# A residual kept in DRAM by token, read back in overlapping rows, in place of four transposes per tile

## The chip, the cores and the metric

The kernel runs on one core of one Trainium2 chip. The metric is the device time of one execution in microseconds. The kernel before took 4258.75 us (median of three runs, 4256.78 to 4262.93). TensorE is called PE below, its weight loads PEld, VectorE DVE, ScalarE ACT, GpSimd POOL, and SyncE, which issues nearly all DMAs, SP.

## The reference

The input is `u`, four sequences (batches) of 1024 tokens with 128 features, in fp32. Four stages follow one another, each as `x = x + layernorm(stage(layernorm(x)))`: a selective state-space scan (called mamba in the code), a mixture of eight experts of which two are chosen per token, a convolution with weights computed per token (31 taps, 16 heads), and a transformer of six layers. The change lies in the last, whose layer is:

```
for i in range(DEPTH):                                   # 6
    x = attn_layer(shift_tokens(x), Wqkv[i], q_scale[i], k_scale[i], Wo[i]) + x
    x = ffn_layer(shift_tokens(x), ln_g[i], ..., W2[i], b2[i]) + x
```

`shift_tokens` delays the upper 64 features by one token. Attention has 16 heads of 64 and is local: the tokens are cut into windows of 32, and a window's queries see the keys and values of its own window and the one before, 64 rows in all. Queries and keys are normalized, scaled and rotated by position. The feedforward part is a layernorm, two 128 x 341 products, a GELU gate and a product back.

## The kernel before, in words

**What is on the chip.** The residual of a batch is held with features on the partitions and tokens along the free axis, in two tiles of 1,186 columns: `hs[b][0]`, called h0, feeds attention, and `hs[b][1]`, called h1, takes its result and feeds the feedforward part. The upper 64 partitions are stored one column to the right, so that a column read straight down is a shifted token. `halves()` (line 1141) names the two halves.

**Tiles and blocks.** Attention goes by tiles of 128 tokens, four windows each: 8 tiles per batch and layer, 192 in all, in the order batch, layer, tile. The feedforward part goes by blocks of 512 tokens, two per batch and layer, 48 in all.

**A tile's steps.**

- `project` (line 1256) multiplies 128 columns of h0 with the query and key weights (four products of 512 columns). ACT squares the results for the norms; DVE multiplies them by the cosine and sine rows of the tile `rot` into `r` and `rb`, POOL adds the two and scales by the inverse root.
- `turn` (line 1314) transposes queries and keys on PE; ACT copies them out as `qT` and `kT`.
- `scores` (line 1328) forms the products of each window's queries and keys (`kT,qT` in the profile), with the mask added by PE; DVE subtracts the maximum, ACT takes the exponential, POOL divides. The result is `at`.
- `mix` (line 1387) needs the values. The value and output weights are multiplied beforehand (`wvo`), so that attention is applied to the residual rows themselves. For that the rows must have tokens on the partitions. `windows` (line 1373) makes them: it transposes 128 columns of h0 on PE for each of four overlapping pieces, 32 tokens apart, into one PSUM bank (`bank<-ident,hs` in the profile), and ACT copies the bank to the tile `xw`. A piece holds four windows of 32 rows, so its rows 0 to 63 serve the even heads of one window and its rows 64 to 127 the odd heads of another; for the first two windows of a tile these are pieces of the tile before, which `mix` gets as `before`. In the first tile of a layer there is no such tile, and two further pieces are turned. Then `at` is transposed to `aT`, the products `aT,xw` (16 instructions a tile) give `zT`, and the products `zT,wvo` (32 instructions) give the attention's result, to which DVE adds h0 into h1.

**A block's steps.** `feedforward` (line 1440) transposes four pieces of h1 on PE (also `bank<-ident,hs` in the profile), normalizes, transposes back, forms three pairs of products with GELU tiles `ge` between, and adds the result to h1 into h0 for the next layer.

**What else runs.** The stages before the transformer for batches 1 to 3 (`mamba`, `chosen_experts`, `conv`) and the preparation of layers 1 to 5 (`prepare_layer`) run beside the tiles, each paced by the number of the tile (`Line`, line 1603). `conv` ends with `finish` (line 1118), which normalizes, transposes and writes h0 for layer 0, for batch 0 one tile at a time and for the others four.

**Order of the work.** Instructions are not issued as the Python code runs. `Order` (line 145) records them as units, finds what depends on what (DRAM by ranges too), and `arrange` (line 278) lays out a schedule with a cost for each kind of unit: 2 us and bytes at 180 GB/s for a DMA, 0.11 us for a transposed piece, and so on. At each step it gives out the unit that can start earliest on its engine, and among those that can start within a short time of it (1 us for DMAs) the one first in program order. It looks ahead by 500 units and assigns the seven shared PSUM banks. Each engine then executes its own list strictly in that order and waits at its head. SP's list holds the DMAs from all stages. All work is recorded in `take` and issued in `give`, so nearly every instruction of the profile has one line, L374; instructions are told apart by their tiles.

**Buffers named below.** `rot` has three buffers, loaded by `load_rot` (line 1237) one tile before its `project`; `xw` two; `ge` two; `eT`, which carries the value and output weights of `prepare_layer` to DRAM, one. `rows` (in DRAM) holds the convolution's input by token; its 30 leading rows are set to zero at the start, in `Common.__init__`, by copies from a zero tile (`rows<-exs` in the profile, the tile being named after its ring). Behind them the same tile fills the experts' lists `listed`, 2.9 MB.

The main loop is `run` (line 1501): `ahead(i + 2)` projects a tile two iterations early, `mix` runs one iteration behind `scores`.

## Time and profile before

| What | Value |
|---|---|
| median of three runs | 4258.75 us (4256.78 to 4262.93) |
| profiled execution, its own time | 4259.06 us |
| its span, first to last instruction | 4257.2 us |
| mean granted TensorE clock | 0.948 |
| PE busy | 3801.6 us |
| DVE busy | 3612.4 us |
| POOL busy | 2964.5 us |
| ACT busy | 2610.7 us |
| bytes moved by DMA | 261.25 MB, 61 GB/s on the mean |

The times are those of one profiled execution. "Busy" counts the time in which an engine executes at least one instruction; matmuls overlap, so that the sum of their durations is more than the busy time, and the time from one group's start to the next group's start tells what a group costs. In a group's line the operands stand as `out<-in`, then shapes and count, then busy time and the mean duration in ns, and behind the bar the idle time of the engine just before these instructions with what ended it. Slices are fortieths of the span, some 106 us each, with a digit for tenths of busy time. In a list of waits a line says which engine, for the instruction that writes the named tile, waited for which engine and tile, with the total in us, the number of times and the longest. `SPq` is SP's list of DMAs. In a timeline a line gives start, duration, engine, operation and tiles, and the count of instructions merged into it.

### The profile page before, as it was taken

What the parts mean: (1) busy time and instruction counts of PE and PEld (TensorE: products, weight loads), DVE (VectorE), ACT (ScalarE), POOL (GpSimd) and SP (SyncE); (2) the same over time, 40 slices, a digit from 0 to 9 for tenths busy, and PEclk for the clock granted to TensorE, in tenths of its full rate; (3) what the DMA queues carried; (4) which work ended last, traced back from release to release, by engine and by line L of the source; (5) the groups of instructions that cost most, each with busy time, mean ns of one, the idle gap of its engine ahead of it and who ended that gap; (6) DMA issues with size and microseconds to landing.
All of it is one profiled execution on the core that took longest, in us unless ns stands there. A gap on an engine that the chain in (4) does not pass through costs nothing. (4 is left out here: it accounts for less than half of the span.)

```text
span 4257.2 us, 112033 instructions
## 1 busy us (share of the span) xinstructions
PE 3801.6 (89%) x45306; PEld 2721.5 (64%) x45317; DVE 3612.4 (85%) x9374; ACT 2610.7 (61%) x4854; POOL 2964.5 (70%) x1832
## 2 busy tenths in 40 slices
PE   3874788998988999988999999999999999999997
PEld 1762465675665666656676677766666777777775
DVE  4668789888997879999998787898989898888985
ACT  3754466675555777655667676666665666666664
POOL 3388667666878766777789665788688666666663
PEclk6886899999998999989999999999999999999998
DMA  3323321222112221111113122121111010101100
GB/s 91 104 83 123 119 85 43 86 62 72 60 68 82 91 73 55 45 57 53 44 63 114 58 65 63 41 73 59 58 61 51 27 41 25 32 21 34 33 27 11
DMA packets 136878, 261.25 MB, mean 61 GB/s; under 512 B 16112, under 2 KB 93992, under 8 KB 129192
## 3 DMA queue, kind: packets, MB, share of 16 engines
q1 hardware_dynamic: 123352, 211.47, 15.0%
q0 software_dynamic: 13008, 42.62, 3.2%
q8 instruction: 357, 5.85, 0.6%
q14 instruction: 161, 1.32, 0.1%
HBM read 224.41 MB, written 29.62 MB: 60 GB/s over the span
## 5 line engine op out<-in xcount | busy, mean ns | idle before, releaser
L374 POOL TENSOR_TENSOR r<-r,rb 128x1024 f32<-128x1024 f32 x384 | 906.9, 2367 | 365.2 <-DVE rb L374 297.9
L374 POOL TENSOR_TENSOR r<-r,root 128x1024 f32<-128x1024 f32 x384 | 723.2, 1903 | 181.2 <-DVE root L374 154.4
L374 PE MATMUL bank<-wqk,hs 128*128 128x512 f32 x1536 | 769.7, 624 | 45.0 <-DVE at L374 13.3
L374 PEld LDWEIGHTS bank<-zT,wvo 128*128 128x128 f32 x6144 | 723.2, 194 | 88.8 <-issue 53.2
L374 PE MATMUL bank<-zT,wvo 128*128 128x128 f32 x6144 | 729.4, 277 | 6.5 <-ACT zT L374 3.5
L374 ACT ACTIVATE sq<-bank 128x512 f32<-128x512 f32 x768 | 450.4, 601 | 458.1 <-DVE words L374 228.1
L374 ACT COPY zT<-bank 128x512 f32<-128x512 f32 x768 | 403.7, 597 | 382.4 <-PE bank L374 376.6
L374 DVE TENSOR_TENSOR r<-bank,rot 128x512 f32<-128x512 f32 x768 | 522.0, 680 | 103.4 <-issue 36.2
L374 POOL TENSOR_TENSOR at<-at,sm 128x1024 f32<-128x1024 f32 x192 | 365.4, 1903 | 326.2 <-DVE sm L374 146.3
L374 DVE TENSOR_TENSOR rb<-bank,rot 128x512 f32<-128x512 f32 x768 | 520.8, 678 | 62.8 <-ACT sq L374 53.8
L374 DVE TENSOR_REDUCE words<-sq 128x8 f32<-128x512 f32 x768 | 526.5, 686 | 14.3 <-ACT sq L374 5.3
L374 PEld LDWEIGHTS bank<-wqk,hs 128*128 128x128 f32 x1536 | 267.6, 195 | 322.7 <-issue 157.7
L374 PE MATMUL bank<-aT,xw 64*128 64x256 f32 x3072 | 430.6, 404 | 25.4 <-DVE at L374 10.3
L374 PE MATMUL bank<-ident,r 128*128 128x128 f32 x3080 | 400.6, 278 | 45.1 <-DVE rb L374 10.0
L374 PEld LDWEIGHTS bank<-ident,r 128*128 128x128 f32 x3080 | 350.1, 143 | 134.9 <-issue 59.7
L374 PEld LDWEIGHTS bank<-aT,xw 64*128 64x128 f32 x3072 | 295.6, 192 | 153.2 <-issue 44.3
L374 PEld LDWEIGHTS bank<-kT,qT 64*32 64x32 f32 x24576 | 259.7, 106 | 106.8 <-issue 105.4
L374 PE MATMUL bank<-kT,qT 64*32 64x64 f32 x24576 | 296.6, 227 | 12.4 <-issue 11.9
L374 DVE TENSOR_REDUCE mx<-bank 128x8 f32<-128x512 f32 x384 | 254.1, 680 | 44.4 <-PE bank L374 44.3
L374 PE MATMUL bank<-fxn,w 128*128 128x512 f32 (+1 forms) x576 | 272.8, 607 | 7.0 <-ACT fxn L374 4.8
L374 ACT ACTIVATE at<-at 128x1024 f32<-128x1024 f32 x192 | 203.5, 1060 | 117.6 <-DVE at L374 83.2
L374 ACT COPY qT<-bank 128x512 f32<-128x512 f32 x384 | 228.3, 600 | 66.2 <-PE bank L374 62.8
(207 smaller groups left out, 6849.8 us busy)
## 6 DMA issues: line engine op xcount, KB each, us to landing
near<-rows SPq DMA_DIRECT2D x31, 1024.0 KB
near<-rows SPq DMA_DIRECT2D x31, 960.0 KB
rot<-rotd SPq DMA_DIRECT2D x192, 128.0 KB
wqk<-in_Wqkv SPq DMA_DIRECT2D x48, 512.0 KB
wvo<-wvod SPq DMA_DIRECT2D x24, 1024.0 KB
ewt<-in_w_ex SPq DMA_DIRECT2D x16, 514.0 KB
w<-in_W SPq DMA_DIRECT2D x24, 341.0 KB
wvod<-eT SPq DMA_DIRECT2D x24, 256.0 KB
```

The source lines that it names most:

```text
L374: getattr(engine, op)(*map(real, args), **{k: real(v) for k, v in kw.items()})
```

## The change

The residual of every layer is also kept in DRAM with one row per token, in a pair of buffers per batch that alternate by layer, with 32 leading rows of zeros. A new function `by_token` turns a block (or a tile, in batch 0 of the convolution's end) once: four transposes on PE into one bank, one ACT copy to a tile `xs` (in the ring of `ge`), one DMA to DRAM. `finish` calls it for layer 0 and `feedforward` for layers 1 to 5. `windows` no longer uses PE and ACT: it reads the four overlapping windows of 64 rows from DRAM, twice, into partitions 0 to 63 and 64 to 127 of `xw`, so that even and odd heads find their own windows and `before` is not needed. It is called for tile i in iteration i, ahead of the mixing of tile i - 1, which uses the `xw` read one iteration earlier. The ring of `rot` goes from three buffers to two. The zero rows of the eight new buffers are filled at the start, between the zero rows of `rows` and the fills of `listed`.

```diff
@@ Common.__init__ @@
+        self.inner = [
+            [dram.tile([WIN + SEQ, D], F32, name=f"inner{b}_{i}") for i in range(2)]
+            for b in range(NB)
+        ]
...
         for rows in self.rows:
             dma(out=rows[:PADL, :], in_=zero[:PADL])
+        for rows in [r for pair in self.inner for r in pair]:
+            dma(out=rows[:WIN, :], in_=zero[:WIN])
@@ Common.finish @@
         for part, dst in halves(self.hs[b][0], j * BLK + ts.start * P, n * P):
             nc.scalar.copy(dst, ps[part][:, : n * P])
+        self.by_token(b, 0, j * BLK + ts.start * P, n)
+
+    def by_token(self, b, l, t0, n):
+
+        c0 = PRE + t0
+        ps = self.transpose4("px", [self.hs[b][0][:, c0 + g * P : c0 + (g + 1) * P] for g in range(n)])
+        xs = self.sb.tile([P, 4, P], F32, "xs", tag="ge", bufs=2)[:, :n, :]
+        self.nc.scalar.copy(xs, ps[:, :n, :])
+        rows = self.inner[b][l % 2][WIN + t0 : WIN + t0 + n * P, :]
+        self.dma(out=rows.rearrange("(g p) d -> p g d", p=P), in_=xs)
@@ Transformer.load_rot @@
-        rot = self.sb.tile([P, 4, DH], F32, "rot", bufs=3)
+        rot = self.sb.tile([P, 4, DH], F32, "rot", bufs=2)
@@ Transformer.windows, mix @@
-    def windows(self, b, t, chunks):
+    def windows(self, b, l, t):
+        xw = self.sb.tile([P, 4, P], F32, "xw", bufs=2)
+        first = self.c.inner[b][l % 2][t * P : t * P + 1, :]
+        src = bass.AP(first.tensor, first.offset, [[D, 2 * WIN], [WIN * D, 4], [1, D]])
+        for e in range(2):
+            self.c.dma(out=xw[e * 2 * WIN : (e + 1) * 2 * WIN], in_=src)
+        return xw
+
+    def mix(self, b, t, at, xw):
         nc, c = self.nc, self.c
-        px = c.bank("px").rearrange("p (g f) -> p g f", f=P)
-        with nc.together(0.11 * len(chunks)):
-            for i, g in enumerate(chunks):
-                c0 = PRE + t * P + (g - 1) * WIN
-                nc.tensor.transpose(px[:, i, :], c.hs[b][0][:, c0 : c0 + P], c.ident)
-        xw = self.sb.tile([P, 4, P], F32, "xw", bufs=2)
-        n = len(chunks)
-        nc.scalar.copy(xw[:, 4 - n :, :], px[:, :n, :])
-        return xw
-
-    def mix(self, b, t, at, before):
-        if before is None:
-            before = self.windows(b, t, (-2, -1))
-        xw = self.windows(b, t, range(4))
...
-                            (xw if e == 0 else xw if g > 1 else before)[rows, (g + 2 * e) % 4, :],
+                            xw[rows, g, :],
@@ Transformer.feedforward @@
+        if l + 1 < DEPTH:
+            c.by_token(b, l + 1, j * BLK, 4)
@@ Transformer.run @@
                 qT = self.turn(projected.pop(i), kT)
+                old, xw = xw, self.windows(b, l, t)
...
-                mixing = self.mix(bm, tm, at, xw if tm else None)
-                xw = next(mixing)
+                mixing = self.mix(bm, tm, at, old if i < len(tiles) else xw)
+                next(mixing)
```

More of the change, by code (lines that the diff above doesn't have):

```diff
@@ L1371, in scores @@
         return at
-    def windows(self, b, t, chunks):
-        nc, c = self.nc, self.c
-        px = c.bank("px").rearrange("p (g f) -> p g f", f=P)
-        with nc.together(0.11 * len(chunks)):
-            for i, g in enumerate(chunks):
-                c0 = PRE + t * P + (g - 1) * WIN
-                nc.tensor.transpose(px[:, i, :], c.hs[b][0][:, c0 : c0 + P], c.ident)
-        xw = self.sb.tile([P, 4, P], F32, "xw", bufs=2)
-        n = len(chunks)
-        nc.scalar.copy(xw[:, 4 - n :, :], px[:, :n, :])
-        return xw
-    def mix(self, b, t, at, before):
-        nc, c = self.nc, self.c
-        if before is None:
-            before = self.windows(b, t, (-2, -1))
-        xw = self.windows(b, t, range(4))
+    def windows(self, b, l, t):
[6 more added lines that the diff above has]
+    def mix(self, b, t, at, xw):
+        nc, c = self.nc, self.c
         aT = self.sb.tile([P, 8, P], F32, "aT", bufs=2)
@@ L1401, in mix @@
             nc.scalar.copy(aT[:, 4 * j : 4 * j + 4, :], pt)
-        yield xw
+        yield
         zT = self.sb.tile([P, 2, 4, 8, WIN], F32, "zT")
@@ L1422, in mix @@
                 )
-        yield xw
+        yield
         py = c.bank("py")
@@ L1437, in mix @@
             nc.vector.tensor_tensor(out=dst, in0=py[rows, :P], in1=src, op=ALU.add)
-        yield xw
+        yield
     def feedforward(self, b, j, l):
```

## The prediction

> **What bounds the kernel now.** I read the page's busy times and slices first, then the windows by stage, then PE's own waits, then the order of time. The page's span, busy line and slices of PE and DVE:
>
> ```profile
> span 4257.2 us, 112033 instructions
> PE 3801.6 (89%) x45306; PEld 2721.5 (64%) x45317; DVE 3612.4 (85%) x9374; ACT 2610.7 (61%) x4854; POOL 2964.5 (70%) x1832
> PE   3874788998988999988999999999999999999997
> DVE  4668789888997879999998787898989898888985
> ```
>
> There are three stretches: a start of 400 us with PE at 4 to 8 tenths, a middle where PE and DVE take turns, and a second half with PE at nine tenths throughout. The view by windows (PE, PEld, DVE, ACT and POOL busy, then the granted clock) puts numbers on the last two:
>
> ```profile
> 400.00:2200.00 1800.00, 1581.26 (x18391) 1112.36 (x18398) 1569.91 (x4063) 1114.38 (x2109) 1317.62 (x827) 0.94 0.21 69
> 2200.00:4150.00 1950.00, 1885.05 (x24521) 1373.55 (x24520) 1717.51 (x4401) 1245.30 (x2266) 1374.17 (x791) 1.00 0.15 49
> ```
>
> From 2200 to 4150 PE is busy 96.7% and DVE 88%; from 400 to 2200 the two are at 88% and 87% and neither bounds alone. PE's own waits from 2200 to 4150 (total, times, longest) are small and scattered:
>
> ```profile
> PE bank L374 <- DVE at L374: 9.2, 11, 2.1
> PE bank L374 <- DVE rb L374: 9.1, 17, 2.1
> PE bank L374 <- ACT qT L374: 8.4, 12, 1.4
> ```
>
> The timeline of PE shows one tile running without a gap, and in it the four pieces that the change removes (`ident,hs`):
>
> ```profile
> 3614.18 1.91 PE L374 MATMUL bank<-ident,r 128*128 128x128 f32 x16
> 3615.93 0.60 PE L374 MATMUL bank<-ident,hs 128*128 128x128 f32 x4
> 3616.37 1.04 PE L374 MATMUL bank<-ident,at 128*128 128x128 f32 x8
> ```
>
> The next group starts 0.44 us after the pieces do; the same gap is 0.44 at 3629.96 and 0.43 at 3645.15. So a set of four costs PE 0.44 us, not the sum of the durations, which overlap.
>
> **The change part by part**
>
> *Turning taken away and put back.* The two groups in question, by form:
>
> ```profile
> L374 PE MATMUL bank<-ident,hs 128*128 128x128 f32 x1008 | 156.5, 280 | 9.5 <-DVE hs L374 3.5 <-DVE at L374 2.2 <-ACT qT L374 1.0
> L374 ACT COPY xw<-bank 128x512 f32<-128x512 f32 x192 | 118.6, 617 | 10.1 <-PE bank L374 8.8 <-DVE rb L374 1.1
> ```
>
> Of 1008 transposes 192 are the feedforward's (48 blocks of 4). The other 816 are the windows: 192 tiles of 4 and 24 first tiles with 2 more. They all go. `by_token` turns each block once per layer: 48 times 4, 192. Net 624 fewer, at 0.44/4 = 0.109 us: 68.0 us of PE at full clock, 0.354 us a tile.
>
> By the number of products `aT,xw` (16 a tile) 78 tiles lie before 2200 us, 109 up to 4150 and 5 behind. Late: 114 tiles by 0.354 is 40.4 us. PE is idle 65 us of those 1950, so nearly every microsecond of PE moves the end; but DVE, at 88%, comes to 90% of the shortened stretch and some waits grow. Bounds 70% and 100%, I take 85%: 34.3 us. Early: 78 by 0.354, at a granted clock of 0.94, is 29.4 us. Here DVE and the chains of other stages hold the end half of the time: bounds 0 and 100%, I take 45%: 13.2 us.
>
> A rule that would forbid this gain: the Trainium skill, "Perfetto Trace Analysis", section "Identifying the Most-Contended Engine", judges TensorE's headroom by the share of its weight loads and not by matmul busy time. By it PE would stand at 1373.55 of 1950, 70%, DVE would be the contended engine, and the sum would be the start's +6 us, against −41.5 by the rows. The gapless tile above speaks for matmul time in this stretch.
>
> *Copies on ACT.* 192 copies (118.6 us) and 24 half ones (9.6) go; 46 of 128x512 at 617 ns and 8 of 128x128 (like `exsT`, 297 ns) come: 97.4 us less on an engine 61% busy. Its waits on PE are its idle time, so I take 0. Bound above: PE's late waits for ACT (about 23 us) vanish. Bound below 0, as ACT's work only shrinks.
>
> *The reads.* 384 reads of 128 KB, two per tile. SP needs 0.32 us for an issue: 384 reads, 54 writes and 8 zero fills are 143 us of an engine that mostly waits. Landing is bounded by the loads of `x` (256 KB in the same 512-byte rows): issued at 0.74 and used at 3.43, 2.7 us; behind megabytes, issued at 14.39 and used at 21.83, 7.4 us. The buffer is free when the products of two tiles before have read it (3607.1) and is needed at 3633.8: 26.7 us of cover against 0.64 + 7.4. I take 0. With the cover gone a read would cost PE what it lies beyond it.
>
> *The write and its read.* The write waits for the ACT copy, the first read for the write's landing. The nearest row: `rows` written at 1056.67, read at 1059.12, 2.45 us, during which SP holds what is queued behind. It follows the block's residual add, whose tile's products come more than a tile (14 us) later; 0 taken, and 48 times 2.45, 118 us, if nothing covered it.
>
> *DMA traffic.* 50.3 MB read and 12.6 MB written, 122,880 packets. The hardware queue now takes 15.0% of 16 engines for 123,352 packets, 0.083 us each; at that rate the share doubles to 30%. Not a bound: 0.
>
> *SP's queue and the rotation ring from three to two.* SP's waits over the whole run:
>
> ```profile
> SPq L374 <- DVE rb L374: 1640.9, 159, 27.8
> SPq L374 <- PE bank L374: 1057.1, 214, 36.3
> ```
>
> SP already stands most of the time before a rotation load that waits for `rb`. With two buffers a load is released by the last `rb` of the tile before (3603.4) and needed by `r` one tile on (3622.4): 19.0 us, where three gave one tile more. Less 0.32 and 7.4, 11.3 us are spare; window reads have 18.7. Behind SP's head stand rotations, weights, windows and the experts' rows; DVE waits for the first, PE for the others. From 3400 on SP's longest wait is 23.6 us. I take 0, since SP's entries follow the planned order of the same events; the bound is a rival below.
>
> *The start.* Eight zero fills come between the four that exist and the large fills. SP's queue and ACT there (start, duration):
>
> ```profile
> 16.11 4.13 SPq L374 DMA_DIRECT2D rows<-exs  x4
> 21.03 5.28 SPq L374 DMA_DIRECT2D listed<-exs  x2
> 26.41 4.42 SPq L374 DMA_DIRECT2D exn<-in_WvT  x1
> ...
> 32.11 5.64 SPq L374 DMA_DIRECT2D wvod<-eT  x2
> ...
> 36.80 0.59 ACT L374 COPY eT<-bank 128x512 f32<-128x512 f32 x1 [17.98 <-DMA wvod<-eT]
> ```
>
> ACT stands 17.98 us before the second `eT`, which waits for a write that SP issues behind these fills; mamba's own copies stand behind it, and PE, DVE and POOL idle. Eight more fills at 0.6 to 1.03 us delay this by 5 to 8 us. Bounds 0 (made good before 400 us) and 8.2; I take +5. In batch 0 `by_token` comes in eight single pieces beside the convolution's chain (hs copied at 243.9, projected from 246.7): +1, bounds 0 and 8 times 0.57 (a transpose and a copy) = 4.6.
>
> **Sum.** −34.3 − 13.2 + 5 + 1 = −41.5 us. The profiled execution took 4259.06 us (span 4257.2 and 1.9 around it), 0.3 above the median of 4258.75; so 4217 us.
>
> **The rivals**
>
> *All of the freed PE time comes back:* −40.4 − 29.4, and at the start +1: 4190. For it: PE's late stretch has no gap and early the copies that go unburden ACT; against it: DVE at 87 and 88%.
>
> *The gain is taken up by DVE:* the freed PE time turns into waits `PE <- DVE at` and `DVE rb`, and only the start's +6 is left: 4265, within the measure. For it: DVE is at 91 to 93% in the windows 1000 to 1300, 1600 to 1900 and 1900 to 2200. Against it: the late stretch, with three fifths of the tiles, where it is at 88%.
>
> *Slower: SP's single queue.* A rotation load or window read is held behind an entry whose engine is late, and DVE's `r` waits for DMA. It decides when holds exceed the spare 11.3 us. If one load in each of the 24 layers meets a hold of the size of SP's longest late wait, 23.6 us, it costs 12.3 us each, 295 us, the far end; if in every third layer, 8 by 12.3 = 98 us against the 41.5 saved: 4315. The point from which it is slower at all is 3.4 such loads. For it: the ring of two, the 1057 us in which SP waits for PE, and one 10.3 us wait of PE for `exs<-listed` already. Against it: no rotation load is waited for anywhere in the trace, though they stand in the same queue.
>
> **How the numbers follow.** A median differing by 0.2% (8.5 us) is about what can be told from no change. The forecast, 4200 to 4240, has 0.50; all of it coming back, below 4200, 0.20; a smaller gain, 4240 to 4250, 0.07; taken up by DVE, 0.09; slower through SP, 0.14. So faster 0.77, same 0.09, slower 0.14. For 8 in 10 the range leaves out a tenth on each side: 4182 (the full gain and some of ACT's 23 us) to 4275 (a little of the third rival); the likeliest case's own is 4200 to 4240.
>
> **What the new profile would show.** Right: `ident,hs` at 384 instructions and PE busy near 3801.6 − 97, as 624 of 1008 rows of 156.5 us go (their overlap counted in); `xw<-bank` gone from ACT, 54 copies to `xs` in its place; tiles of the late stretch 0.35 us closer; the second `eT` at 42 to 45 us. No engine waits on `xw` or `rot` by DMA. Wrong: lines such as `DVE r <- DMA rot` or `PE bank <- DMA xw` with more than some 10 us in total; PE waits on DVE after 2200 us up by 30 or more; or tiles farther apart because the planned order itself differs, which no row of this trace prices and which would break the forecast in either direction.

## The result: 1.4% slower, and the profile after

The changed kernel took 4317.82 us (median of four runs, 4312.42 to 4324.13), the kernel before beside it 4257.76 us (4252.15 to 4262.93): a ratio of 1.0136, 95% interval 1.0118 to 1.0154. Forecast were 4217 us and a range up to 4275. The profiled execution took 4317.51 us. Its span, busy line and hardware DMA queue, from the page of the changed kernel:

```profile
span 4315.7 us, 111685 instructions
...
PE 3805.1 (88%) x44676; PEld 2659.9 (62%) x44693; DVE 3608.5 (84%) x9374; ACT 2547.4 (59%) x4698; POOL 2964.4 (69%) x1832
...
q1 hardware_dynamic: 253624, 274.54, 20.0%
```

There are 630 matmul records fewer, and PE is busy for as long as before (3805.1 us; the forecast had it near 3801.6 − 97). The groups say that the work has gone; what is left of `ident,hs`, the longest group beside it, and SP's new DMAs with their issue times (minimum, median and longest in ns), all of the changed kernel:

```profile
L374 PE MATMUL bank<-ident,hs 128*128 128x128 f32 x384 | 64.9, 286 | 13.8 <-DVE hs L374 7.1 <-ACT hs L374 4.5 <-DVE rb L374 0.8
...
L374 PE MATMUL bank<-wqk,hs 128*128 128x512 f32 x1536 | 788.5, 630 | 39.3 <-DVE at L374 8.9 <-DVE m L374 7.9 <-DVE rb L374 4.8
```

```profile
L374 SPq DMA_DIRECT2D xw<-inner x384: 573/579/1850, 251.9 to 4256.3; - x192
L374 SPq DMA_DIRECT2D inner<-ge x54: 319/382/1266, 250.1 to 4190.2; - x54
L374 SPq DMA_DIRECT2D inner<-exs x8: 302/365/422, 20.0 to 25.3; - x8
```

`ident,hs` lost 91.6 us of records (156.5 before), but the records of the other groups grew: `wqk,hs` by 18.8, `aT,xw` by 21.7, `ident,r` by 9.7. So the busy time of PE did not fall with its work, and does not tell by itself how much room PE has.

The windows by stage (same columns as in the prediction; the cuts after the first are put 60 us later):

```profile
400.00:2260.00 1860.00, 1614.48 (x18379) 1105.02 (x18391) 1595.69 (x4123) 1110.94 (x2079) 1347.40 (x846) 0.93 0.26 82
2260.00:4210.00 1950.00, 1862.04 (x23942) 1326.20 (x23942) 1695.37 (x4358) 1192.93 (x2152) 1346.99 (x776) 0.99 0.21 66
```

In the late 1950 us, where most of the gain was forecast, PE is 23 us less busy than before (1885.05), but the tiles follow no faster, as the table below shows; what PE no longer does, it waits, for several engines (the longest of these waits; total, times, longest; 2260 to 4210 us of the changed kernel):

```profile
PE bank L374 <- POOL at L374: 14.5, 27, 1.7
PE bank L374 <- DVE at L374: 13.7, 14, 3.6
PE bank L374 <- issue: 9.1, 19, 1.6
```

No engine waits for a read of `xw` or for `rot`. The only waits for a new DMA are these two of ACT:

```profile
ACT ge L374 <- DMA inner<-ge: 2.5, 2, 2.2
ACT L374 <- DMA inner<-ge: 2.3, 2, 1.2
```

They look too small to matter, 4.8 us together. They are the trail to the cause. The moment at which each tile's products `zT,wvo` start, read from the traces, shows where the 60 us arise (us behind the kernel before, whose own start is in the second column; "tie alone" and "own buffer" are two of the experiments below):

| tile | before, us | changed kernel | tie alone | own buffer |
|---|---|---|---|---|
| 0 | 428 | -4.9 | +10.3 | -2.2 |
| 30 | 1173 | +11.1 | +6.3 | +7.4 |
| 36 | 1294 | +43.1 | +30.0 | +10.8 |
| 72 | 2091 | +30.9 | -1.5 | +8.2 |
| 78 | 2208 | +42.9 | +23.8 | +5.9 |
| 120 | 3000 | +45.5 | +22.6 | +0.2 |
| 126 | 3116 | +56.5 | +47.8 | -0.8 |
| 186 | 4147 | +60.8 | +54.2 | -5.3 |

The loss comes in steps, near tiles 35, 77 and 124, and between tiles 126 and 186 little changes: none of the gain forecast for these late tiles appears (60 by 0.354 us, 21 us). Part of the first step is made good again: by tile 72 the changed kernel has 12 us of it back, and the tie alone all of it. Against the run with an own buffer the steps are clearer: 32 us at tile 36, 23 at 72, 37 at 78, 45 at 120, 57 at 126 and 66 at 186. Near these tiles three of the six pieces of the convolution for later batches end (`finish`), beside the transformer. (The kernel before runs at slightly different speeds on different chips, medians of 4245 to 4263 us, so the last two columns may hold some 12 us of that by the end; the experiments are compared by ratios to the kernel before on the same chip.)

ScalarE's timeline at the first step names the event (changed kernel; start, duration, operation):

```profile
1241.12 0.69 ACT L374 ACTIVATE ge<-bank,b 128x512 f32<-128x512 f32 x1
1245.71 0.68 ACT L374 ACTIVATE ge<-bank,b 85x512 f32<-85x512 f32 x1 [3.90 <-DVE pd L374]
...
1266.20 1.17 ACT L374 COPY hs<-bank 64x512 f32<-64x512 f32 x2
...
1271.24 0.58 ACT L374 COPY ge<-bank 128x512 f32<-128x512 f32 x1 [1.72 <-PE bank L374]
...
1275.65 1.28 ACT L374 ACT_TABLE_LOAD   x1
1276.95 0.69 ACT L374 ACTIVATE ge<-bank,b 128x512 f32<-128x512 f32 x1
```

Two of the three GELU operations of a feedforward run at 1241 and 1246; the remaining one only at 1277. Between them stands, at 1271.24, a copy into a buffer of the same ring: it is `xs` of the convolution's end, in `by_token`. A ring of two buffers is handed out in program order. Here `xs` stands just ahead of the feedforward's three GELUs (in the 18th feedforward between the first and the second), so the GELU two places behind it, the second of the three, takes the same buffer again. It gets it only after the convolution has transposed, copied `hs`, transposed again, copied `xs` and stored it; the third, 85 wide, takes the other buffer and ran before it. In the view of the waits this is nearly invisible, since the order written out for ACT already has the GELU behind the copy: ACT does other work in between, and nobody is recorded as waiting for it.

### The profile page after: what moved, and what is told of

It is laid out like the page before. It is cut to its first block, busy times and chain, and to the rows that moved or that the text cites. A ratio compares the mean times of both kernels' runs of the same rounds, so it can differ in the third digit from the quotient of the medians.

```text
span 4315.7 us, 111685 instructions
## 1 busy us (share of the span) xinstructions
PE 3805.1 (88%) x44676; PEld 2659.9 (62%) x44693; DVE 3608.5 (84%) x9374; ACT 2547.4 (59%) x4698; POOL 2964.4 (69%) x1832
## 5 line engine op out<-in xcount | busy, mean ns | idle before, releaser
L374 PE MATMUL bank<-wqk,hs 128*128 128x512 f32 x1536 | 788.5, 630 | 39.3 <-DVE at L374 8.9
L374 DVE TENSOR_TENSOR r<-bank,rot 128x512 f32<-128x512 f32 x768 | 524.1, 682 | 117.2 <-PE bank L374 45.5
L374 PE MATMUL bank<-aT,xw 64*128 64x256 f32 x3072 | 452.3, 410 | 44.9 <-DVE at L374 21.8
L374 PE MATMUL bank<-ident,r 128*128 128x128 f32 x3080 | 410.3, 280 | 56.1 <-POOL r L374 25.4
L374 PEld LDWEIGHTS bank<-aT,xw 64*128 64x128 f32 x3072 | 301.4, 194 | 194.9 <-issue 45.1
```

What stands on the lines that cost most here:

```text
L374: getattr(engine, op)(*map(real, args), **{k: real(v) for k, v in kw.items()})
```

## The experiments

Ratios are to the kernel before on the same chip, with 95% intervals. "Tie" means that the convolution's `xs` and the feedforward's GELU share the ring `ge`.

### Where the loss comes from

**The changed kernel with a buffer of the convolution's own for `xs`.**

```diff
-        self.by_token(b, 0, j * BLK + ts.start * P, n)
+        self.by_token(b, 0, j * BLK + ts.start * P, n, "cxT", 1)
...
-    def by_token(self, b, l, t0, n):
+    def by_token(self, b, l, t0, n, tag="ge", bufs=2):
...
-        xs = self.sb.tile([P, 4, P], F32, "xs", tag="ge", bufs=2)[:, :n, :]
+        xs = self.sb.tile([P, 4, P], F32, "xs", tag=tag, bufs=bufs)[:, :n, :]
```

> The changed kernel, but by_token called at the end of the convolution puts xs into the convolution's own buffer cxT instead of the ring ge of the feedforward part. Theory 4, the shared ring ties the side stage's end to the main line's GELU tiles, in an order fixed by the program, and the list of every engine pays for it: some 30 us faster than the changed kernel, a ratio to before near 1.007. Theory 5, the added work itself (turning, copies, DMAs) costs: within 8 us of the changed kernel, ratio 1.012 to 1.014.

Measured: 4250.98 us against 4246.74, ratio 1.0011 (1.0001 to 1.0020). Nearly the whole loss is gone, with all transposes, copies, reads and writes of the change in place. (The order of the instructions is laid out anew here too; more on that below.) The same feedforward's GELUs, in ACT's timeline of this run:

```profile
1237.40 1.26 ACT L374 ACTIVATE ge<-bank,b 128x512 f32<-128x512 f32 x2
1241.99 0.68 ACT L374 ACTIVATE ge<-bank,b 85x512 f32<-85x512 f32 x1 [3.33 <-DVE pd L374]
```

From the first GELU to the last, that feedforward (the 8th of 48) takes 4.6 us here and 35.8 in the changed kernel; the 18th takes 7.9 against 31.4, the 30th 5.7 against 27.1. That is 76 us of stretching in three places, at the three steps of the table. What the held feedforward costs the engines is seen in windows over these three stretches (PE, PEld, DVE, ACT, POOL busy); first the changed kernel, then the run with an own buffer at its corresponding times:

```profile
1245.00:1277.00 32.00, 23.61 (x384) 17.14 (x384) 23.21 (x74) 19.47 (x35) 8.03 (x9) 0.92 0.24 71
2138.00:2162.00 24.00, 19.04 (x235) 13.41 (x236) 18.90 (x82) 16.13 (x31) 7.39 (x8) 0.93 0.18 54
3058.00:3081.00 23.00, 18.28 (x348) 13.12 (x347) 16.75 (x66) 16.94 (x30) 8.64 (x6) 0.97 0.33 102
```

```profile
1241.00:1273.00 32.00, 28.78 (x408) 19.79 (x408) 29.95 (x95) 20.23 (x39) 9.95 (x6) 0.92 0.15 44
2115.00:2139.00 24.00, 21.92 (x232) 14.04 (x232) 23.03 (x80) 15.11 (x28) 10.76 (x8) 0.93 0.15 47
3013.00:3036.00 23.00, 21.32 (x329) 13.90 (x328) 19.71 (x70) 14.39 (x30) 8.12 (x6) 1.00 0.24 70
```

PE is busy 60.9 of 79 us in the changed kernel and 72.0 in the other; DVE 58.9 and 72.7. Layer by layer, the next attention needs the feedforward's result, and while that is held the two engines run out of work. These windows hold only 11 us (PE) to 14 us (DVE) of the loss; more of it follows behind them, when the late layer starts: from the products of tile 33 to those of tile 36 the changed kernel takes 80 us (1257 to 1337), the run with an own buffer 51 (1253 to 1304).

**The kernel before with the tie alone.** The converse, with almost no work: one column of 128 numbers is copied into a buffer of the ring and stored.

```diff
@@ finish, in the kernel before @@
+        tie = self.sb.tile([P, BLK], F32, "tie", tag="ge", bufs=2)
+        nc.scalar.copy(tie[:, :1], ps[:, :1])
+        self.dma(out=self.tied[k], in_=tie[:, :1])
```

> The kernel before, complete, with the tie of the two buffers alone added: at the end of each convolution piece a buffer of the GELU's ring of two is taken, ScalarE copies one column into it and one DMA of 128 x 4 bytes stores it in a DRAM tensor that nothing reads. No rows by token are written or read, the windows are transposed as before. Theory of the tie (the feedforward's GELU waits for the convolution's end because both take the same two buffers in program order): most of the loss comes back, 25 to 65 us over the kernel before, 4283 to 4323 us. Rival (the loss lies in the copies, the rows or the reads, and the own buffer of the earlier run helped only by another order): a few small copies and stores cost 0 to 10 us, 4258 to 4268 us.

Measured: 4306.82 us against 4246.01, ratio 1.0143 (1.0127 to 1.0158). Fourteen copies of 0.16 us and as many stores cost 61 us, as much as the whole change. ACT's timeline at the second step, the store in SP's, and what PE waited for behind it:

```profile
2121.94 1.17 ACT L374 COPY hs<-bank 64x512 f32<-64x512 f32 x2 [0.58 <-PE bank L374]
2123.12 0.16 ACT L374 COPY ge<-bank 128x1 f32<-128x1 f32 x1
...
2132.39 1.28 ACT L374 ACT_TABLE_LOAD   x1 [6.27 <-DMA tied<-ge]
2133.68 0.69 ACT L374 ACTIVATE ge<-bank,b 85x512 f32<-85x512 f32 x1
```

```profile
2123.31 0.33 SPq L374 DMA_DIRECT2D tied<-ge  x1
```

```profile
2134.42 0.80 PE L374 MATMUL bank<-aT,xw 64*128 64x256 f32 x2 [6.31 <-ACT ge L374]
```

Here the hold shows openly: the GELU's table load waits 6.27 us for the store of the tiny tie, the GELU follows, and PE stands 6.31 us. The 8th, 18th and 30th feedforwards take 45.1, 36.3 and 14.9 us between their first and last GELU (4.6, 4.2 and 2.7 in the kernel before). The steps of the table lie at the same tiles as in the changed kernel, but the first, with the longest hold, is made good by tile 72; what stays comes from the other two. Taken away alone and added alone, the tie is worth 53 and 61 us: it is the cause of the loss. That the two amounts are so near each other is not to be read closely. In the tie alone the GELU's table load starts 9.1 us after the issue of the store (2123.31 to 2132.39), in the changed kernel, at its first step, 3.8 us after (1271.85 to 1275.65).

**The changed kernel with three buffers for `rot`.**

```diff
-        rot = self.sb.tile([P, 4, DH], F32, "rot", bufs=2)
+        rot = self.sb.tile([P, 4, DH], F32, "rot", bufs=3)
```

> The changed kernel with three rotation buffers as before. Theory 3, the shorter ring delays rotation loads behind SP's head: most of the 60 us come back, 4260 to 4280. Theories 1 and 2: 4318, within 10.

Measured: 4297.88 against 4245.22, ratio 1.0118 (1.0096 to 1.0140), where the changed kernel had 1.0136. The third buffer brings some 8 us, within the two intervals, and does not explain the loss.

**The kernel before in another planned order.** Its work is complete; the schedule is laid out as if the windows cost nothing.

```diff
-        with nc.together(0.11 * len(chunks)):
+        with nc.together(0.0):
...
-        nc.scalar.copy(xw[:, 4 - n :, :], px[:, :n, :])
+        nc.scalar.copy(xw[:, 4 - n :, :], px[:, :n, :]).cost = 0.0
```

> The kernel before with all of its work, but the planner is told that the window transposes and their copies cost nothing; so only the order of instructions changes, in the way in which the change alters it. Theory 1 (order): it moves by more than 20 us, and slower, 4280 to 4320. Theory 2 (the freed time is worth nothing, order is not the cause): within 10 of 4258.

Measured: 4253.62 against 4245.22, ratio 1.0018 (1.0009 to 1.0028). Leaving the windows out of the plan costs 8 us. The order of the changed kernel itself, which also has the new work in it, is not tested by this.

### What TensorE's freed time is worth

**The kernel before with its windows planned but not issued.** Every other instruction keeps its place; `xw` holds a constant, so the windows are left out.

```diff
-                nc.tensor.transpose(px[:, i, :], c.hs[b][0][:, c0 : c0 + P], c.ident)
+                nc.tensor.transpose(px[:, i, :], c.hs[b][0][:, c0 : c0 + P], c.ident).ghost = True
...
-        nc.scalar.copy(xw[:, 4 - n :, :], px[:, :n, :])
+        nc.scalar.copy(xw[:, 4 - n :, :], px[:, :n, :]).ghost = True
@@ Order.give @@
+            if u.ghost:
+                continue
```

> The kernel before, with its order of instructions kept to the letter: the window transposes and their copies are planned as before but left out when the instructions are issued, and xw holds a constant set once (so attention mixes constants, and the output is not the reference's). Theory 1, the freed time of PE and ACT is worth what the forecast said and the loss comes from the new order: 4190 to 4218 us. Theory 2, the freed time is worth nothing since waits for DVE and POOL end last in every tile: 4245 to 4262.

Measured: 4232.10 against 4245.22, ratio 0.9966 (0.9951 to 0.9982). Leaving out 816 transposes at 0.109 us, 89 us of PE, and the copies on ACT brings 14 us: 16%. The timeline of PE in the late stretch shows what became of the time:

```profile
3591.63 1.91 PE L377 MATMUL bank<-ident,r 128*128 128x128 f32 x16
...
3594.77 1.49 PE L377 MATMUL bank<-kT,qT 64*32 64x64 f32 x128
3596.80 2.00 PE L377 MATMUL bank<-aT,xw 64*128 64x256 f32 x16 [0.54 <-issue]
...
3605.83 1.91 PE L377 MATMUL bank<-ident,r 128*128 128x128 f32 x16
```

In this tile PE stands 0.54 us before `aT,xw`, about what the transposes had cost, and the period from `ident,r` to `ident,r` is 14.20 us: no shorter than the 14.03 us of the tile of the kernel before that the prediction showed (from 3614.18 to the next `ident,r` at 3628.21). Over tiles 110 to 185 the mean period by the two traces is 17.43 us here and 17.44 before. The engine that PE stands for is not named (`issue`), but the windows of the two tiles, first the kernel before, show a second engine that is full:

```profile
3614.18:3628.21 14.03, 14.03 (x216) 11.12 (x215) 13.66 (x33) 9.03 (x17) 11.58 (x8) 1.00 0.04 11
```

```profile
3591.63:3605.83 14.20, 13.66 (x212) 11.00 (x211) 13.71 (x33) 8.52 (x16) 11.63 (x8) 1.00 0.04 12
```

In the tile without a gap on PE, DVE was busy 13.66 of 14.03 us, 97%. The 88% of the late stretch is a mean over tiles like this one and others. Without the transposes PE is busy 13.66 us and DVE 13.71 of the 14.20: by these records such a tile had no more than 0.4 us to give, whatever was taken off PE.

**The kernel before with VectorE relieved.** Two of a tile's four multiplications `rb` cover four heads of eight; every instruction keeps its place. Part of the rotation is left out.

```diff
+                m = 4 if j == 1 else 8
                 nc.vector.tensor_tensor(
-                    out=rb[:, hd, :].rearrange("p h (k d) -> p h k d", k=2),
-                    in0=swapped(ps),
+                    out=rb[:, 8 * j : 8 * j + m, :].rearrange("p h (k d) -> p h k d", k=2),
+                    in0=swapped(ps)[:, :m],
```

> The kernel before, its order kept, with DVE freed instead of PE: of each tile's four multiplications into rb, the two for the later heads are done on 4 of 8 heads (the other columns keep zeros set at the start, so the rotation is incomplete), planned at full cost. By the pitch of 0.60 us for 512 and 0.40 for 256 elements this frees 0.40 us of DVE per tile, 77 us in all, about as much as the window pieces are of PE (89). Theory 2, DVE's chain ends last in most tiles: 40 us or more faster than before. The forecast's theory, PE ends last: less than 15 us faster.

Measured: 4191.61 against 4246.74, ratio 0.9867 (0.9849 to 0.9885). The page has DVE busy 3518.6 us, 94 less than in the kernel before (more than the 77 us of the expectation, which goes by the distance of instructions), for 56 us gained: 60%, or 73% of the 77. For PE in the run above the same two measures give 21% (67 us off its busy time, 3734.4 us on the page) and 16%. By either, a freed microsecond of DVE is worth some three to four and a half of PE, although PE shows 97% busy in the late stretch and DVE 88%.

**The changed kernel with its own buffer, three `rot` buffers and late fills; the same with products beside.** The first moves the eight zero fills behind the two large ones:

```diff
-        for rows in [r for pair in self.inner for r in pair]:
-            dma(out=rows[:WIN, :], in_=zero[:WIN])
...
                 in_=zero[:, None, :].to_broadcast([P, MAXT, D]),
             )
+        for rows in [r for pair in self.inner for r in pair]:
+            dma(out=rows[:WIN, :], in_=zero[:WIN])
```

> As the run with an own buffer and three buffers for the tables, and the eight fills of the first rows with zeros are issued behind the two large fills of the expert lists and not ahead of them. If the fills ahead are what delays the first second-half work by 4.4 us, and that delay is carried to the end: 3 to 6 us below that run, 4249 to 4257 us, at or just below the kernel before. If the delay is taken up on the way: within 2 us of that run.

Measured: 4242.64 against 4246.01, ratio 0.9997 (0.9988 to 1.0006). Without the late fills:

> The changed kernel with the convolution's rows copied into a buffer of the convolution's own instead of the GELU's ring, and with three buffers for the rotation tables, as before the change. Theory of the tie, with the tables' third buffer worth the 8 us that it was worth alone: ratio 0.999 to 1.0005, 4254 to 4260 us. Rival (with the tie gone the tables' buffers no longer matter, the two overlap): ratio 1.0005 to 1.002, 4260 to 4266 us. The windows' transposes that are gone (68 us of TensorE) bring next to nothing in both, since VectorE's chain ends last; by the theory of the prediction (TensorE's time counts 85% late) it would be below 4225 us.

Measured: 4245.80 against 4246.01, ratio 0.9998 (0.9989 to 1.0007). So the third `rot` buffer is worth some 5 us beside the own buffer (1.0011 to 0.9998, intervals that just overlap), and the fills' place cannot be told from nothing. Stripped of these side effects, the change neither gains nor loses. At 16% the 68 us of PE should have left 11 us, 0.26%, and that is not seen either.

The next run loads PE in the order of the late-fills kernel: 384 products into columns that nobody reads, given no time in the plan. (The order of the other instructions is the same in both traces, on every engine.)

```diff
         with nc.together(3.65):
+            for rows, src in halves(h0, t * P, P):
+                nc.tensor.matmul(
+                    py[rows, P : 2 * P], c.ident[rows, rows], src,
+                    start=True, stop=True, skip_group_check=True,
+                )
```

> The changed kernel with an own buffer, three table buffers and late fills, complete, with the 384 products beside in columns that nobody reads, all other work in exactly the order of the kernel without them (the products are planned at no time). They take 0.37 us of TensorE a tile (a group of them in the trace of the run before: 3625.91 to 3626.28), 71 us in 192 tiles. If TensorE has the time to spare that the change gave it: ratio 0.999 to 1.003, and the 48 us of the run before were the order's. If TensorE's added time counts in the late tiles (64 x 0.37 = 24 us) and half of it early: ratio 1.008 to 1.013, as the run before.

Measured: 4260.77 against 4248.99, ratio 1.0029 (1.0021 to 1.0038), 0.32% or 14 us above the kernel without the products. They take 71 us of PE by the distance of instructions: 19% counts. Added or freed, a microsecond of PE is worth 0.16 to 0.19, as long as the order stays; each of the two has an uncertainty of some 0.07 by the intervals. The late stretch (2200 to 4150 us) without and with the products:

```profile
2200.00:4150.00 1950.00, 1877.14 (x24342) 1338.48 (x24341) 1722.28 (x4430) 1207.29 (x2180) 1384.76 (x797) 1.00 0.21 67
```

```profile
2200.00:4150.00 1950.00, 1907.14 (x24619) 1344.51 (x24618) 1716.89 (x4411) 1201.51 (x2173) 1377.94 (x794) 1.00 0.22 67
```

PE takes 30 us more in a stretch that already showed 96%, and DVE does nearly as much as without.

**Freed PE and relieved DVE together.** The edit that relieves VectorE, on the late-fills kernel; part of the rotation is left out.

> The changed kernel with an own buffer, three table buffers and late fills, and two of the four multiplications rb of each tile done on four heads of eight instead of all eight, as in the run on the kernel before that freed 77 us of VectorE and gained a ratio of 0.9867 (part of the rotation is left out; the rest is complete). If TensorE's freed time begins to count once VectorE is relieved: ratio 0.977 to 0.984. If not (the rest of VectorE's chain still ends last): 0.985 to 0.988, as before without the change.

Measured: 4196.86 against 4258.93, ratio 0.9849 (0.9836 to 0.9863). The kernel before with the same relief had 0.9867; the difference of 0.18%, 8 us, lies within the two intervals, which overlap. DVE's relief brings 63 us here (3596.5 to 3501.1 us busy, 95 less: 66%), and PE's freed time stays worth little.

### What the planned order is worth

**The products beside, with their time in the plan.** The same work as above, but the plan has 4.2 us for the group instead of 3.65, so that the whole order comes out differently.

```diff
-        with nc.together(3.65):
+        with nc.together(4.2):
```

> The changed kernel with an own buffer, three table buffers and late fills (0.9997), complete, VectorE adding the residual as ever, and the same 384 products computed besides into columns that nobody reads: TensorE alone is loaded, by 50 us busy as measured in the run with the residual on TensorE. If TensorE has time to spare that the change gave it: within 8 us, ratio 0.999 to 1.0015. If TensorE's added time counts 85%, as the prediction read it: 40 us more, ratio 1.008 to 1.011.

Measured: 4309.05 against 4263.13, ratio 1.0109 (1.0094 to 1.0125). The reading of "added time counts 85%" would have fitted, and it would have been wrong: in the unchanged order the same products cost 0.32%, so 0.8%, 34 us, is the order's.

**Two plans with other costs.** The changed kernel laid out with costs nearer to the measured ones on DVE and ACT, and the kernel before with 0.225 us for every small operation on DVE:

```diff
-            return 0.07 + n * 1.04e-3, 0.10
+            return 0.15 + n * 1.04e-3, 0.10
         if engine == "scalar":
-            return 0.25 + n * (0.45e-3 if n <= 512 else 0.7e-3), 0.12
+            return 0.32 + n * (0.55e-3 if n <= 512 else 0.72e-3), 0.12
```

> The changed kernel, planned with costs nearer to the trace: 0.08 us more for every DVE instruction (0.68 us for 512 elements instead of 0.60) and 0.60 instead of 0.48 us for an ACT copy of 512. Theory 1, with the planner's too short DVE and ACT costs as the reason that its order stalls: below 4258, about 4220. Theory 2: 4290 to 4320, since no order helps.

Measured: 4337.61 against 4245.22, ratio 1.0202 (1.0171 to 1.0233).

```diff
-            return 0.07 + n * 1.04e-3, 0.10
+            return max(0.225, 0.07 + n * 1.04e-3), 0.10
```

> The kernel before, planned with 0.225 us for a small DVE instruction, the distance at which they follow each other in the trace, instead of 0.10 for 32 elements. Theory 2 (DVE ends last, and the planner does not know it): it changes the order, and for the better, 4200 to 4245 by a before of 4258. If the order is not sensitive to this: within 10 of before.

Measured: 4330.08 against 4246.74, ratio 1.0194 (1.0177 to 1.0211). Both missed. The second has no tie and only the kernel before's work: an order alone can cost 1.9%. The first has the tie, and its 18th feedforward takes 43 us between its first and last GELU; beyond that, why these orders are worse stays open. It limits what can be said of the tie, too: each of its two runs also has an order of its own. What speaks for the tie and not for chance is that the loss vanishes with it and appears with it by a like amount, and that the steps lie, in both runs that have it, at the three feedforwards that its copies hold.

**The change's work in the order of the kernel before,** with three `rot` buffers and the own buffer for `xs`; with the tie, or with two `rot` buffers, that order is not possible at all.

Every unit that the kernel before also has keeps its place (`line`, a stack for each engine, the next on top); the reads, the `xs` transposes and copies and the writes (`fresh`) are put where they first can be.

```diff
@@ Order.arrange @@
+        old = [u for u in units if not u.new]
+        line = {e: [] for e in self.LAG}
+        for k, u in sorted(enumerate(old), key=lambda f: -place[f[0]]):
+            line[u.engine].append(u)
...
+                heads = [u for u in line[e][-1:] if not u.left] + fresh[e]
...
@@ load_rot, by_token @@
-        rot = self.sb.tile([P, 4, DH], F32, "rot", bufs=2)
+        rot = self.sb.tile([P, 4, DH], F32, "rot", bufs=3)
-        xs = self.sb.tile([P, 4, P], F32, "xs", tag="ge", bufs=2)[:, :n, :]
+        xs = self.sb.tile([P, 4, P], F32, "xs", tag=tag, bufs=bufs)[:, :n, :]
```

> The whole change, in the order of instructions of the kernel before: each engine issues what both kernels share in exactly the old order (the window pieces left out), and the new turning, copies, writes and reads are put in as soon as they are ready. Rotation ring of three, xs of the convolution in cxT, since the old order is impossible with the shorter and the shared ring. Theory 4 (order): ratio to before 0.997 to 1.002. Theory 5 (the added work itself): 1.008 to 1.014.

Measured: 4264.21 against 4246.74, ratio 1.0037 (1.0022 to 1.0051). That is 16 us. By the traces it is 7 us behind at the first tile and again at tile 186; but the kernel before in the table ran on a chip on which it takes 12 us longer, so the rest of the 16 us comes up along the way. In the same order of PE, DVE and POOL, and on a chip of nearly the same speed, leaving the windows out had gained 14 us. So the change's own work takes this gain back and 16 us more, and no run shows which part of it does.

### Attempts at a gain

**The convolution's rows written straight from its tile `y`,** which has them by token, with no transposes, copy or ring (with the own buffer's tie gone and three `rot` buffers):

```diff
-        self.by_token(b, 0, j * BLK + ts.start * P, n)
+        r0 = WIN + j * BLK + ts.start * P
+        for e in range(2):
+            f = slice(e * (D // 2), (e + 1) * (D // 2))
+            rows = self.inner[b][0][r0 + e : r0 + e + n * P, f]
+            self.dma(out=rows.rearrange("(g p) d -> p g d", p=P), in_=y[:, :, f])
```

> As the run with an own buffer and three buffers for the tables, but the convolution's end writes its rows straight from the tile y that it has by token, in two DMAs of half rows, the second half one row later as the token shift wants, with no transposes, no copy and no buffer of a ring; the feedforwards' rows stay as in the changed kernel. Theory of the tie: the copy and the transposes (32 of 192 transposes, 11 of 51 copies at most) lie where nothing waits, so it is as the run with an own buffer, within 6 us: 4250 to 4264 us. Rival (the side work itself costs where it is put): 8 to 15 us faster than that run, 4243 to 4250 us.

Measured: 4258.65 against 4246.01, ratio 1.0029 (1.0018 to 1.0040). Less work and 0.3% slower than the run with an own buffer and three `rot` buffers; whether by the order or by the DMAs of 256-byte rows was not separated.

**The attention's residual added on TensorE,** to spend its free time on DVE's behalf:

```diff
-        with nc.together(3.65):
+        with nc.together(4.2):
...
+            for rows, src in halves(h0, t * P, P):
+                nc.tensor.matmul(
+                    py[rows, :P], c.ident[rows, rows], src,
+                    start=False, stop=True, skip_group_check=True,
+                )
-        for (rows, src), (_, dst) in zip(halves(h0, t * P, P), halves(h1, t * P, P)):
-            nc.vector.tensor_tensor(out=dst, in0=py[rows, :P], in1=src, op=ALU.add)
+        for rows, dst in halves(h1, t * P, P):
+            nc.scalar.copy(dst, py[rows, :P])
```

> The changed kernel with an own buffer, three table buffers and late fills; besides, the attention's residual is added on TensorE: two products with the identity over 64 rows each go into the projection's sum, and ScalarE copies the two halves out, where VectorE added them (384 additions of 284 ns, 109 us, leave VectorE; TensorE gets 384 products more, at most 0.28 us each or 107 us; ScalarE 384 copies at some 0.4 us, 154 us). Theory that VectorE's chain ends last: by the exchange rate of the run that freed 77 us of VectorE (55 us gained) 70 to 80 us gained, less about 15 to 30 for TensorE: ratio 0.983 to 0.990. Rival, the prediction's reading (TensorE is at its limit late, its time counts 85%): 0 to 20 us lost, ratio 1.000 to 1.005.

Measured: 4254.27 against 4258.93, ratio 0.9991 (0.9982 to 1.0000): a miss for the theory of VectorE. The same edit on the kernel before:

> The kernel before, windows transposed as ever, with the same residual on TensorE. Theory that VectorE's chain ends last, TensorE's next: a gain too, but smaller by what TensorE's 68 us are worth once VectorE is relieved, 10 to 40 us: ratio 0.988 to 0.997. If TensorE's time is spare even then, the same ratio as the changed kernel's within 0.2%. By the prediction's reading it is 58 us slower than that run, ratio 1.013 to 1.02.

Measured: 4269.02 against 4258.93, ratio 1.0026 (1.0017 to 1.0035): 15 us above the run on the changed kernel, the one place where the 68 us of PE show a little of their worth (22%, the orders being different). And on the changed kernel with the two products left out, the group planned at 3.65 us again, and the copies kept, so that the residual is missing:

```diff
-            for rows, src in halves(h0, t * P, P):
-                nc.tensor.matmul(
-                    py[rows, :P], c.ident[rows, rows], src,
-                    start=False, stop=True, skip_group_check=True,
-                )
```

> As the run with the residual on TensorE, without the two products: the attention's residual is left out, ScalarE copies the projection's two halves. VectorE has its 109 us less, TensorE nothing more, ScalarE the copies (412 copies into hs in that run, 262 ns each). If TensorE's products took the gain: ratio 0.980 to 0.986. If the copies took it (ScalarE's turn comes later than VectorE's, and the next projection and the feedforward wait for hs): ratio 0.996 to 1.000.

Measured: 4192.54 against 4263.13, ratio 0.9841 (0.9826 to 0.9857). The copies on ACT take little: 109 us of additions off DVE (384 of 0.28 us) bring 66 us, 61%. By the page DVE's busy time falls by 71 us only (3596.5 to 3525.4), and of these 93% arrive; the other two relief runs had 60 and 66% by that measure. The products with their new plan took 64 us of that. In an unchanged order such products cost 14 us, in a plan with 4.2 us for their group 48; so most of what was lost is by the order, but for this pair itself that is argued, not shown.

No kernel that does all the work was clearly faster than the kernel before: the lowest ratio, 0.9991, has 1.0000 at the end of its interval.

## Why the prediction was wrong

It failed twice, by two separate steps.

**The gain: a mis-sized term.** The step was "PE is idle 65 us of those 1950, so nearly every microsecond of PE moves the end ... I take 85%", and 45% early; together −47.5 of 69.8 us (40.4 + 29.4). The part of the mechanism that held: the transposes went (384 left, as forecast), at 0.109 us each. The share was wrong: in an unchanged order 16% of freed and 19% of added PE time reached the end. The gapless tile was read as speaking for PE; it shows only that PE was occupied, and DVE was too, 13.66 of its 14.03 us. "DVE, at 88%" was a mean over the stretch and hid this. The rule weighed in the prediction, by which TensorE's headroom is judged by its weight loads (and by its share of the peak arithmetic, which was not worked out here) and not by matmul busy time (the Trainium skill, "Perfetto Trace Analysis", "Identifying the Most-Contended Engine"), pointed the right way here: it named DVE as the contended engine, and 94 us off DVE gained 56 us where 89 us off PE gained 14. Its sum for the change, the start's +6 alone, lies near the kernel without the tie (1.0011, +4 to 5 us), but that is luck: with a third `rot` buffer and the same late start, that kernel is at 0.9998. The rival "the gain is taken up by DVE", 4265 us, had the mechanism of this half and got 0.09; its sign, PE's late waits for DVE, is weak (`DVE at` 9.2 to 13.7 us, `DVE rb` 9.1 to 6.4), since other engines stand among the releasers.

**The loss: a term that was never set.** The step was the copies on ACT: "Bound below 0, as ACT's work only shrinks". That bounds work, not order. `xs` takes a buffer of the GELU's ring, as the diff says in so many words, and this was costed nowhere. A ring with two users hands out its buffers in program order, so the convolution, a side stream that may be late, stands in front of the feedforward, the main stream. It cost 53 to 61 us, some five times the 11 us that the freed time could bring (68 us by 0.16). The kernels without the tie do not show even these 11 us (0.9997); what takes them is open.

**The other terms.**

- The start: forecast +5, second `eT` at 42 to 45 us. SP's queue and ACT in the changed kernel:

```profile
19.99 5.77 SPq L374 DMA_DIRECT2D inner<-exs  x8
...
36.42 5.71 SPq L374 DMA_DIRECT2D wvod<-eT  x2
```

```profile
41.17 0.58 ACT L374 COPY eT<-bank 128x512 f32<-128x512 f32 x1 [22.25 <-DMA wvod<-eT]
```

  36.80 became 41.17: +4.4. Right in size; whether it reaches the end no run shows. The first tile's products start 4.9 us earlier than before all the same, and with the fills moved the second `eT` still starts at 40.53.
- The reads, the write before the read, the DMA traffic, each taken as 0: right, no wait for `xw` in the trace. The issue of a read was taken as 0.32 us and took 0.58, so that the new DMAs hold SP for some 384 x 0.579 + 54 x 0.382 + 8 x 0.365 = 246 us instead of 143; no wait for `xw` or `rot` came of it. The queue's share rose to 20.0% and not to 30%: packets of the new kind cost less than the mean of the old (5.0% of 16 engines' span for 130,272 more, 0.027 us each).
- ACT: forecast -97 us busy, measured -63; without effect as taken.
- The `rot` ring: taken as 0, worth some 5 to 8 us, at the edge of what the intervals can tell.
- The rival "SP's single queue" ended on the right side with the wrong mechanism; its 4315 us for a hold in every third layer is near the 4318 measured by luck. It would have shown as waits for `rot` or `xw`, and there are none. SP's waits behind PE did grow:

```profile
SPq L374 <- PE bank L374: 1836.5, 489, 36.0
SPq L374 <- DVE rb L374: 923.0, 149, 11.5
SPq L374 <- ACT ge L374: 139.8, 30, 19.0
```

- The planned order was named as what would break the forecast in either direction, and got no room in the range. Orders of equal work lie up to 1.9% apart here, 80 us: more than anything that was priced.

## What to carry to other kernels

When an edit puts a tile into a ring that another stream uses, price the ring and not the copy: ask who takes the next buffer in program order, and how late the new user can be. A timeline without gaps does not make an engine the bound; see whether another engine is just as full in the same stretch, then take something from it, or add something to it, in an unchanged order, and see what share of the time comes through. Where a schedule is laid out anew with every edit, compare kernels in one order before a difference below 2% is put down to the edit.

## What was not expected of the hardware

- The issue of a read into 64 partitions of four 512-byte rows each held SP 0.579 us (median of 384), the store of a tile by token 0.382 (median of 54).
- The recorded busy time of PE stayed (3801.6 and 3805.1 us) when 68 us of transposes were taken away. With the tie gone it fell by 30 us (3771.2 in the run with late fills), and with the windows of the kernel before not issued by 67 of 89 us (3734.4). The tie alone raised it by 27 us (3828.7) without one matmul more.
- An engine at 88% by its records was nearer to setting the pace than one at 97%: the share of a freed busy microsecond that arrived was 0.60, 0.66 and 0.93 on DVE (three runs) and 0.21 on PE. In a tile without gaps on PE, DVE was at 97% too.
- A hold of tens of microseconds on one stream left 4.8 us in the list of waits, since an engine with a fixed order does other work before the late instruction and is never seen waiting for it.
